# Short products that nothing reads, in the last group of a Perceiver layer, with a new planned order

## The chip, the cores and the metric

The kernel runs on one core of a Trainium2 chip. The metric is device time in microseconds: the median of several executions. The profile is one further execution, recorded by the hardware profiler. The names used below: PE is TensorE (matrix products), PEld its weight loads, DVE is VectorE, ACT is ScalarE, POOL is GpSimd and SP is SyncE, which here only issues DMAs. Each engine works through its own instructions in order; between engines they wait for each other through semaphores.

## What is computed

One Perceiver layer in float32 for 64 sequences: x is 64 × 64 × 256 and the context is 64 × 256 × 256. All three parts have a residual.

```python
def _layernorm(x, axis=-1, eps=1e-05):
    m = jnp.mean(x, axis=axis, keepdims=True)
    v = jnp.var(x, axis=axis, keepdims=True)
    return (x - m) / jnp.sqrt(v + eps)
...
x = x + _L0_xattn_ref(_layernorm(x), ctx_1024, ctx_1024, Wq, bq, Wk, bk, Wv, bv, Wo, bo)
x = x + _L0_attn_ref(_layernorm(x), w_qkv, b_qkv, w_out, b_out)
x = x + _L0_ffn_ref(_layernorm(x), w_gate, w_up, w_down)
```

The first part is cross-attention with 16 heads of 16: q from x, k and v from the context, softmax(q kᵀ / 4) v, then Wo and bo. The second is causal self-attention with the same heads. The third is a feed-forward net with quantized operands: weights are rounded to −1, 0, 1 times a scale, and activations to 8 bits with a scale per token:

```python
def _act_quant(x):
    scale = 127.0 / jnp.clip(jnp.max(jnp.abs(x), axis=-1, keepdims=True), 1e-05)
    xq = jnp.clip(jnp.round(x * scale), -128.0, 127.0) / scale
    return x + jax.lax.stop_gradient(xq - x)
...
gate = jax.nn.silu(_bitlinear(x, w_gate))
up = _bitlinear(x, w_up)
return _bitlinear(gate * up, w_down)
```

## The kernel before

The 64 sequences are worked in nine groups: seven of eight and, at the end, two of four (GB; NG is their number). A group of eight is four tiles of 128 tokens, a group of four is two. Cross-attention goes by pairs of sequences, since one context load (cT, 512 KB) holds two. Self-attention and the feed-forward net go by groups. The groups overlap: while one is in its feed-forward net, the next ones are in their attentions.

No loop sets the order of instructions. The functions describe operations (`op`) with an engine, an estimated duration, a due time `at`, and the buffers that they read and write. `Graph.run` then places them one by one, before the kernel is built: for each engine it takes the ready operation with the lowest due time, with small penalties for waiting (LATE), for a change of PE's mode (STICK) and for another ACT table (TURN), among those not further than AHEAD past the oldest operation not yet placed. SHIFT adds a fixed number to the due times of operations of one kind ("PE sc", "DVE hq f"), and LAST adds another past the due time END. For loads it reckons a landing time from their size. The result is a fixed order on every engine, and a fixed order of DMA issues on SP. Nothing is decided while the kernel runs. DMAs are dealt in turn to eight semaphore lanes, and an issue waits until the earlier DMA of its lane has landed. ACT issues the small loads at the start (bk_c, ident, par, qpar, bq_c, sel, bqk_c, causal, two bv_c, two brow); SP issues the rest.

What the steps below touch:

- The start. `load_x` (L357), `load_weights` (L361) and `load_ctx` (L366) issue from SP. PE runs 20 rows of products of ones (L939) that nothing reads, then k_a (L484, context times Wk), v_a (L519, context times Wv), tp_a (L470, transposes of the normalized x) and q_a (L484).
- A norm. `stats` (L433, L434) on DVE for each tile, giving mv; `root` (L443 to L451), eight short instructions on POOL, giving rstd and newton; `apply` (L459) on ACT for each tile, giving xn; then transposes on PE.
- `out_bias` (L367) works out the bias that goes with Wo: a DVE copy of the bv_c column into rep_bo (L372), two products on PE, and a DVE addition. `add_bias` (L550, POOL) adds it to x.
- Cross-attention for a pair: sc (L607, PE), its row maximum nm (L620, DVE), msl and mtp, scT (L638 and L643, PE), the exponentials PT (L648, ACT), av (L656, PE), keep (L677, L679, DVE).
- Self-attention: ssc (L725, PE); then, for each of two head halves and four j, mask (L737, DVE), smax (L740, DVE), less (L742, POOL), sexp (L744, ACT), stot (L748, DVE), over (L752, POOL), stp (L760, PE), spT (L765, ACT); then sav (PE), o_s (L541, PE) and x with its statistics (L545, L433, DVE).
- Feed-forward: root and apply as above; `scales` (amax_x, qunit_x, qscale_x, units; L819 to L858) and `rounded` (L862) on DVE; q (L869, DVE); its transposes qtp (L836, PE) and qT (L840, ACT). For each tile of tokens and each half of the 1024 columns: gate and up (L882, PE), silu (L889, ACT), h (L892, DVE). Then amax_hf (L819), hscaled (h_f, L908, ACT), hq (L911, DVE), hqtp (PE), hqT (ACT), down (L919, PE), x (L923, DVE). After the last tile of a group, SP stores it (L930).

PE tiles that hold products lie in PSUM: "mm" is a ring of four slots, `tile_of` takes one.

Of the kernel before, what the change touches and what calls it, by code (L numbers as in the profile page):

```python
# [39 lines left out]
P = 128  # L40
D = 256
H = 16
E = D // H
KC = D // P
# [3 lines left out]
T = 64  # L48
# [3 lines left out]
NG = len(GB)  # L52
# [43 lines left out]
class Op:  # L96
# [12 lines left out]
SETTLE = {"PE": 230.0, "ACT": 180.0, "DVE": 150.0, "POOL": 100.0, "SP": 0.0}  # L109
SELF = {"PE": 0.0, "ACT": 120.0, "DVE": 118.0, "POOL": 120.0, "SP": 0.0}  # L110
MODE = 93.0
STICK = 0.0005
TABLE = 1283.0
AHEAD = 5.691
HURRY, SPURT = 2.4886, 8
WAIT = 578031
LATE = 0.0129
TURN = 2.8858
WARM = 10
TURNS = 2  # L120

SHIFT = {
    "ACT exp": -0.11, "ACT hqT f": -10.14, "ACT hscaled f": 1.99, "ACT k s": 0.18, "ACT keep": -0.9,
    "ACT mT": 1.22, "ACT norm a": 0.11, "ACT norm f": -2.03, "ACT norm s": 2.98, "ACT q s": -0.85,
    "ACT qT f": -11.74, "ACT sexp s": -0.59, "ACT silu f": -0.43, "ACT skeep s": 1.07, "ACT spT s": -3.21,
    "ACT turned a": -1.44, "ACT v a": -2.48, "ACT v s": -0.49, "DVE h f": 0.9, "DVE hq f": 0.13,
    "DVE hscales f": 1.37, "DVE mask s": 0.027, "DVE nm": 0.73, "DVE q f": 2.75, "DVE ratio": 0.51,
    "DVE rounded f": 3, "DVE smax s": 0.07, "DVE stats a": -2.45, "DVE stats f": -3.39, "DVE stot s": 0.805,  # L130
    "DVE wdown sums": 1.47, "DVE x a": -1.84, "DVE x f": 1.05, "DVE x s": 1.31, "PE av": -0.29,
    "PE down f": -0.64, "PE gate/up f": 0.1, "PE k a": 0.05, "PE mtp": 0.12, "PE q a": -0.24,
    "PE q s": 0.03, "PE sav s": -1.58, "PE sc": -0.38, "PE ssc": -0.13, "PE stp s": 0.21,
    "PE turn a": -0.11, "PE turn s": -1.7, "PE v a": -0.1, "PE v s": 2.11, "PE wgate total": 0.98,
    "POOL less s": -1.59, "POOL root a": 2.36, "SP load wgate": 1.56, "SP load wup": 1.17,
    "SP load x": -6.63,
}

LAST = {
    "ACT exp": -2.03, "ACT hqT f": 9.14, "ACT hscaled f": 1.51, "ACT keep": -0.53, "ACT mT": -2.79,  # L140
    "ACT norm s": -5.27, "ACT qT f": 9.17, "ACT sexp s": -1.13, "ACT silu f": 1.38, "ACT spT s": 2.36,
    "ACT v a": 3.26, "ACT v s": 1.58, "DVE h f": -0.28, "DVE hq f": 1.39, "DVE hscales f": 1.92,
    "DVE mask s": -1.27, "DVE nm": -2.37, "DVE q f": -2.35, "DVE ratio": 1.17, "DVE rounded f": -1.88,
    "DVE smax s": 0.59, "DVE stats f": 1.64, "DVE stats s": 2.35, "DVE stot s": -0.66, "DVE syT s": -0.92,
    "DVE x f": 2.71, "DVE x s": -2.93, "PE down f": 3.91, "PE gate/up f": 0.21, "PE hqtp f": 2.44,
    "PE k a": 3.27, "PE mtp": 1.86, "PE o s": -2.39, "PE sc": -0.79, "PE ssc": -1.18, "PE stp s": -0.27,
    "PE v a": -1.05, "PE v s": -1.66, "POOL less s": 2.66,
}
END = 59.061


def kind(eng, name):
# [4 lines left out]
class Graph:  # L157
# [52 lines left out]
    def run(self, emit=True):  # L210
# [8 lines left out]
        for o in self.ops:  # L219
            if o.chain[0] is o:  # L220
                heads[o] = outside(o)
                if not heads[o]:
                    able[o.eng].append(o)
        table, mode, landed = None, "", 0.0
        waiting = sorted(self.ops, key=lambda o: o.at)
        done, first, order = set(), 0, []

# [24 lines left out]
        while len(done) < len(self.ops):  # L252
            while waiting[first] in done:
                first += 1
            limit = waiting[first].at + AHEAD
            best = None
            for e, ops in able.items():
                found = [(t, o) for t, o in ((start(o), o) for o in ops if o.at <= limit)
                         if t is not None]
                if not found:  # L260
                    continue
                soon = min(t for t, _ in found)
                t, o = min(((t, o) for t, o in found if t <= soon + WAIT),
                           key=lambda f: f[1].at + LATE * (f[0] - soon)
                           + STICK * (e == "PE" and f[1].mode != mode)
                           + TURN * (e == "ACT" and f[1].table not in (None, table)))
                if best is None or t < best[0]:
                    best = t, o
            if best is None:
                raise RuntimeError("no operation can go: " + ", ".join(  # L270
                    o.name for ops in able.values() for o in ops))
            t, head = best
            able[head.eng].remove(head)
            for o in head.chain:
                done.add(o)
                t = max(t, o.ready)
                for b in o.uses:
                    if b.slot is None and b.ring:
                        b.ring.to_come -= 1
                        f, _, k, b.ring = slots(b)[0]  # L280
                        t = max(t, f)
                        b.ring.held[k], b.slot = b, k
                        if emit:
                            b.t = b.ring.make(k, b)
                ns = o.ns
                if o.table and o.table != table:
                    table = o.table
                    ns += TABLE
                if o.eng == "PE" and o.mode != mode:
                    mode = o.mode  # L290
                    ns += MODE
                end = t + ns
                if o.bytes:
                    landed = max(landed, t + 1900.0) + o.bytes / 330.0
                for n in o.after:
                    seen = landed if o.bytes else end + (SELF if n.eng == o.eng else SETTLE)[o.eng]
                    n.ready = max(n.ready, seen)
                    n.missing -= 1
                    if n.chain is not o.chain:
                        h = n.chain[0]  # L300
                        heads[h] -= 1
                        if not heads[h]:
                            able[h.eng].append(h)
                for b in o.uses:
                    b.users -= 1
                    b.end = max(b.end, landed if o.bytes else end + SETTLE[o.eng])
                    if b.ring and not b.users:
                        b.ring.free[b.slot] = b.end
                o.start, o.end = t, end
                order.append(o)  # L310
                if emit:
                    o.emit()
                t = end
            free[head.eng] = t
# [12 lines left out]
def dve(n):  # L327
    return 65.0 + 1.044 * n


def pool(n):
    return 20.0 + 1.92 * n


def layers(nc, a, out, R, c):

    g_ = Graph()
    op = g_.op
# [11 lines left out]
    def tile_of(name, dtype=F32):  # L350
        return bufs("mm", [P, 512 if dtype == F32 else 1024], name, dtype)
# [7 lines left out]

    def load_weights(at, w, name):  # L360
        op("SP", 60, at, f"load {name}", lambda: nc.sync.dma_start(w.t, a[name]), writes=[w],  # L361
           size=KC * D * 4 * P)

    def load_ctx(bp, at):
        cT = cTs[bp] = bufs("cT", [P, KC, 2 * S], f"cT_{bp}")
# [182 lines left out]
    def add_bias(at, x, bias, i0):  # L548
# [3 lines left out]
            ALU.add), reads=[bias] + [(x, i) for i in range(i0, i0 + k)],  # L552
           writes=[(x, i) for i in range(i0, i0 + k)])


    def prepare(g, at, width):

# [129 lines left out]
    def self_attention(g, at, width):  # L687
        nm, x, yTa = f"s{g}", xs[g], yTs[g]
# [44 lines left out]
        def softmax(hg, j, sc, t, k):  # L733
# [5 lines left out]
                c["causal"].unsqueeze(1).to_broadcast(full), ALU.add), reads=[sc], writes=[t])  # L739
            op("DVE", dve(nt), p(k), f"smax {nm}", lambda: nc.vector.tensor_reduce(  # L740
                mx.t, t.t, AX.X, ALU.max), reads=[t], writes=[mx])
            op("POOL", pool(nt), p(k), f"less {nm}", lambda: nc.gpsimd.tensor_tensor(  # L742
                t.t, t.t, mx.t.unsqueeze(2).to_broadcast(full), ALU.subtract), reads=[mx], writes=[t])
            op("ACT", act(nt) + 40, p(k + .5), f"sexp {nm}", lambda: nc.scalar.activation(  # L744
# [2 lines left out]
            def total():  # L747
                nc.vector.reduce_sum(tot.t, t.t, axis=AX.X)  # L748
                nc.vector.reciprocal(tot.t, tot.t)

            op("DVE", dve(nt) + 218, p(k + 1), f"stot {nm}", total, reads=[t], writes=[tot])
            op("POOL", pool(nt), p(k + 1), f"over {nm}", lambda: nc.gpsimd.tensor_tensor(  # L752
                t.t, t.t, tot.t.unsqueeze(2).to_broadcast(full), ALU.mult), reads=[tot], writes=[t])

# [45 lines left out]
        for hg in range(KC):  # L800
            k = 12 + 5 * hg
# [41 lines left out]
    def ffn(g, mv, at, width):  # L843
        nm, x = f"f{g}", xs[g]
        ni = x.shape[1]
        (wg, g_unit), (wu, u_unit), (wd, d_unit) = (weights[k] for k in ("gate", "up", "down"))
        p = lambda k: at + width * k / 14
        y = root(p(0), mv, ni, nm)
        xn = bufs("xn", [P, ni, D], f"xn_{nm}")
        for i in range(ni):  # L850
            apply(p(1), x, y, xn, i, nm)
        (amax, scale, unit), emit_scale = row_scale(xn, ni, f"x{g}")
        u = bufs("units", [P, 2, ni], f"units_{g}")

# [5 lines left out]
        def rounded():  # L860
# [4 lines left out]
        q = bufs("q", [P, ni, D], f"q_{nm}", BF16)  # L865
        op("DVE", dve(ni * D) + 680, p(2), f"scales {nm}", scales, reads=[xn, g_unit, u_unit],
           writes=[amax, scale, unit, u])
        op("DVE", ni * 262, p(2.2), f"rounded {nm}", rounded, reads=[scale], writes=[xn])
        op("DVE", 40 + ni * 140, p(2.4), f"q {nm}", lambda: nc.vector.tensor_scalar(  # L869
            q.t, xn.t, MAGIC, 127.0, ALU.subtract, ALU.min), reads=[xn], writes=[q])  # L870

# [248 lines left out]
```

## Time and profile before

| | us |
|---|---|
| three runs | 861.82, 861.9, 863.13 |
| median | 861.9 |
| the profiled execution | 862.48 |
| its span | 860.7 |
| PE busy | 831.4 |
| DVE busy | 690.3 |
| ACT busy | 590.4 |
| POOL busy | 301.0 |

The profiled execution's time of 862.48 holds its span, 860.7, and 1.8 us that lie outside the records. Its mean granted TensorE clock is 0.99 of full speed. A busy share is an average over the whole span, so the profile is read by stretches. In a line of the timeline the first number is the start in us, the second the duration, then follow engine, line of the code, operation, output<-input, sizes and how many instructions the row holds; in brackets is the idle time ahead of it and what ended that.

### The profile page before, as it was taken

How to read it: one execution, taken by the hardware profiler on the slowest of the kernel's cores; microseconds unless marked ns; L12 is line 12 of the kernel's file. 1: busy time of each engine (PE TensorE's matmuls, PEld its weight loads, DVE VectorE, ACT ScalarE, POOL GpSimd, SP SyncE). 2: the span in 40 equal slices, each digit the busy share in tenths (PEclk: the TensorE clock that was granted, in tenths of full speed). 3: DMA queues.
4: the chain of work that ended last, by engine and by line, in shares of the span. 5: the costliest groups of instructions: out<-in, count | busy, mean ns of one | idle time of the engine just before them, and what ended most of it. 6: DMA issues, size and time to landing. Idle time of an engine off the chain costs nothing. (4 is left out here: it accounts for less than half of the span.)

```text
span 860.7 us, 28167 instructions
## 1 busy us (share of the span) xinstructions
PE 831.4 (97%) x12136; PEld 573.2 (67%) x12136; DVE 690.3 (80%) x1499; ACT 590.4 (69%) x948; POOL 301.0 (35%) x505
## 2 busy tenths in 40 slices
PE   8999899999999999999999999999999999998966
PEld 5766657776577756676667766777567775776633
DVE  2587678896888878988789886889779877999995
ACT  3554666547986597747886487865888487767855
POOL 3330527424242334405144152422344141354640
PEclk9999999999999999999999999999999999999988
DMA  7212201002022210222112111211012320011110
GB/s 264 76 51 100 75 27 51 27 3 62 14 51 64 57 40 6 51 88 39 38 38 51 39 39 39 50 58 51 8 39 51 64 38 14 14 27 39 26 37 38
DMA packets 47740, 41.82 MB, mean 49 GB/s; under 512 B 39168, under 2 KB 39680, under 8 KB 47616
## 3 DMA queue, kind: packets, MB, share of 16 engines
q1 hardware_dynamic: 45888, 39.59, 17.5%
q8 instruction: 95, 1.56, 0.7%
q10 hardware_dynamic: 1728, 0.43, 0.2%
q14 instruction: 29, 0.24, 0.1%
HBM read 26.65 MB, written 4.19 MB: 36 GB/s over the span
## 5 line engine op out<-in xcount | busy, mean ns | idle before, releaser
L620 DVE TENSOR_REDUCE nm<-sc 128x8 f32<-128x2048 f32 x64 | 144.7, 2261 | 27.9 <-PE sc L607 27.9
L648 ACT ACTIVATE PT<-scT 128x1024 f32<-128x1024 f32 x128 | 125.1, 1020 | 28.4 <-PE scT L643 28.1
L484 PE MATMUL k_a<-cT,wk 128*128 128x512 f32 x256 | 122.7, 609 | 2.5 <-DMA wk<-in_wk_dram 2.5
L519 PE MATMUL v_a<-wv,cT 128*128 128x256 f32 x512 | 122.6, 383 | 0.0
L682 POOL TENSOR_TENSOR yT_a<-keep 128x128 f32<-128x128 f32 x64 | 30.7, 480 | 247.7 <-DVE keep L679 189.0
L519 PEld LDWEIGHTS v_a<-wv,cT 128*128 128x128 f32 x512 | 95.0, 190 | 19.6 <-issue 3.2
L742 POOL TENSOR_TENSOR s_s<-s_s,smax_s 128x512 f32<-128x512 f32 (+1 forms) x72 | 67.3, 951 | 60.5 <-DVE smax_s L740 56.8
L507 ACT ACTIVATE kT<-k_a,bk_c 128x512 f32<-128x512 f32 x64 | 43.9, 685 | 59.4 <-PE k_a L484 59.1
L656 PEld LDWEIGHTS av<-PT,v 128*32 128x32 f32 x4096 | 60.4, 110 | 28.6 <-ACT PT L648 13.0
L484 PEld LDWEIGHTS k_a<-cT,wk 128*128 128x128 f32 x256 | 46.4, 192 | 47.5 <-issue 39.0
L752 POOL TENSOR_TENSOR s_s<-s_s,stot_s 128x512 f32<-128x512 f32 (+1 forms) x72 | 67.1, 952 | 27.6 <-DVE msl L613 12.3
L607 PE MATMUL sc<-kT,qm 32*128 32x256 f32 x1024 | 73.3, 400 | 3.0 <-ACT PT L648 3.0
L643 PE MATMUL scT<-qm,kT 32*128 32x128 f32 x2048 | 75.1, 270 | 0.0
L677 DVE SCALAR_TENSOR_TENSOR keep<-av,par,keep 128x256 f32<-128x256 f32 x64 | 30.6, 479 | 53.6 <-ACT keep L672 43.7
L656 PE MATMUL av<-PT,v 128*32 128x64 f32 x4096 | 71.4, 221 | 2.0 <-ACT PT L648 1.8
L643 PEld LDWEIGHTS scT<-qm,kT 32*128 32x128 f32 x2048 | 68.5, 186 | 0.2
L679 DVE RECIPROCAL keep<-keep 128x128 f32<-128x128 f32 x64 | 61.0, 953 | 2.2
L607 PEld LDWEIGHTS sc<-kT,qm 32*128 32x128 f32 x1024 | 46.2, 184 | 19.8 <-ACT PT L648 5.8
L737 DVE TENSOR_TENSOR s_s<-ssc,causal 128x512 f32<-128x512 f32 (+1 forms) x72 | 42.7, 620 | 13.4 <-PE ssc L725 13.2
L892 DVE SCALAR_TENSOR_TENSOR h_f<-up_f,units,silu_f 128x512 f32<-128x512 f32 x64 | 46.5, 739 | 7.7 <-ACT silu_f L889 6.3
L550 POOL TENSOR_TENSOR x<-x,bo_r 128x512 f32<-128x512 f32 x32 | 40.1, 1272 | 32.6 <-issue 16.7
L525 ACT COPY v<-v_a 128x512 f32<-128x512 f32 x64 | 37.2, 582 | 20.9 <-PE v_a L519 20.8
(156 smaller groups left out, 1677.6 us busy)
## 6 DMA issues: line engine op xcount, KB each, us to landing
cT<-in_ctx_dram SPq DMA_DIRECT2D x32, 512.0 KB, 3.4
x<-in_x_dram SPq DMA_DIRECT2D x7, 512.0 KB, 3.7
out_dram<-x SPq DMA_DIRECT2D x7, 512.0 KB, 2.8
wffn_gate<-in_wgate_dram SPq DMA_DIRECT2D x2, 512.0 KB, 5.8
wffn_up<-in_wup_dram SPq DMA_DIRECT2D x2, 512.0 KB, 5.7
wffn_down<-in_wdown_dram SPq DMA_DIRECT2D x2, 512.0 KB, 3.7
wqkv<-in_wqkv_dram SPq DMA_DIRECT2D x1, 768.0 KB, 7.4
x<-in_x_dram SPq DMA_DIRECT2D x2, 256.0 KB, 2.6
```

What stands on the lines that cost most here:

```text
L484: nc.tensor.matmul(pm.t[:, 0:n], w.t[:, kc, c0:c0 + P], src.t[:, kc, :], start=(kc == 0), stop=(kc == KC - 1))
L507: op("ACT", act(n) + 100, at, f"k {name}", lambda: nc.scalar.activation(kT.t[:, hg, :], pm.t[:, 0:n], AF.Identity, bias=bias), reads=[pm], ...
L519: nc.tensor.matmul(pm.t[:, i * D:(i + 1) * D], src.t[:, kc, (i0 + i) * P:(i0 + i + 1) * P], w.t[:, kc, c0:c0 + D], start=(kc == 0), stop=( ...
L607: nc.tensor.matmul(sc.t[:, j, hg, :], q(hg, j), kT.t[rows(j), hg, k0:k0 + S], start=True, stop=True)
L620: op("DVE", dve(NJ * KC * S), at, f"nm {n}", lambda: nc.vector.tensor_reduce(nm.t, sc.t, AX.X, ALU.max, negate=True), reads=[sc], writes=[nm])
L643: nc.tensor.matmul(sT.t[:, j, hg, s * P:(s + 1) * P], kT.t[rows(j), hg, k0 + s * P:k0 + (s + 1) * P], q(hg, j), start=False, stop=True, sk ...
L648: op("ACT", act(NJ * S), at + .03, f"exp {n}", lambda: nc.scalar.activation(pT.t[:, hg].rearrange("p j k n -> p j (k n)"), sT.t[:, :, hg, ...
L656: nc.tensor.matmul(av.t[rows(j), h, hg, :], v.t[:, ((n % 2) * SC + s) * NP + hg * NJ + j, 2 * h:2 * h + 2, :].rearrange("p a e -> p (a e)" ...
L679: nc.vector.reciprocal(t.t[:, 1], t.t[:, 1])
L742: op("POOL", pool(nt), p(k), f"less {nm}", lambda: nc.gpsimd.tensor_tensor(t.t, t.t, mx.t.unsqueeze(2).to_broadcast(full), ALU.subtract), ...
L752: op("POOL", pool(nt), p(k + 1), f"over {nm}", lambda: nc.gpsimd.tensor_tensor(t.t, t.t, tot.t.unsqueeze(2).to_broadcast(full), ALU.mult), ...
L892: op("DVE", dve(512) + 60, p(k), f"h {nm}", lambda: nc.vector.scalar_tensor_tensor(h.t[:, n0:n0 + 512], up.t, u.t[:, 1, i:i + 1], sl.t, AL ...
```

## The change

A new function makes one PE operation of one product of the identity with a value that another engine has just made (the row maxima or sums of a softmax, or a mean and variance, an inverse root, a normalized tile, a scale), and of four bf16 products of 128 × 128. They go to a "mm" tile that nothing reads. It is called in the last group alone: in self-attention after smax and after stot for even j (eight times), and in the feed-forward net after mv, after the root, after xn, after the scales and after the rounding (five times). That makes 13 operations and 65 products.

```diff
+BRIDGE = 4
...
+    def kept_warm(at, name, src, rhs):
+
+        pt = tile_of(f"warm_{name}_{len(g_.ops)}")
+
+        def emit():
+            nc.tensor.matmul(pt.t[:, 0:rhs().shape[-1]], c["ident"], rhs(), start=True, stop=True)
+            for k in range(BRIDGE):
+                nc.tensor.matmul(pt.t[:, P:2 * P], c["sel"][:, 0, :], c["ident16"], start=True, stop=True)
+
+        op("PE", 330, at, f"bridge {name}", emit, reads=[src], writes=[pt])
...
+            if g == NG - 1 and j % 2 == 0:
+                kept_warm(p(k), nm, mx, lambda: mx.t)
...
+            if g == NG - 1 and j % 2 == 0:
+                kept_warm(p(k + 1), nm, tot, lambda: tot.t)
...
+        final = g == NG - 1
+        if final:
+            kept_warm(p(0), nm, (mv, ni - 1), lambda: mv.t[:, ni - 1, :])
...
+        if final:
+            kept_warm(p(.5), nm, y[0], lambda: y[0].t)
+            kept_warm(p(1.5), nm, (xn, ni - 1), lambda: xn.t[:, ni - 1, 0:T])
...
+        if final:
+            kept_warm(p(2.1), nm, scale, lambda: scale.t)
...
+        if final:
+            kept_warm(p(2.3), nm, xn, lambda: xn.t[:, ni - 1, 0:T])
```

The planner is told other numbers. The load of wqkv is counted with its real size, three times what it was; the first landing is reckoned from 3,000 ns on, and the rate is 300 bytes per ns instead of 330. Its constants change a little, and all of SHIFT and LAST is new.

```diff
-STICK = 0.0005
+STICK = 0.0002
...
-AHEAD = 5.691
-HURRY, SPURT = 2.4886, 8
-WAIT = 578031
-LATE = 0.0129
-TURN = 2.8858
+AHEAD = 6.0713
+HURRY, SPURT = 2.4951, 8
+WAIT = 180501000.0
+LATE = 0.0126
+TURN = 2.8337
...
-END = 59.061
+END = 59.2063
...
-        table, mode, landed = None, "", 0.0
+        table, mode, landed = None, "", 3000.0
...
-                    landed = max(landed, t + 1900.0) + o.bytes / 330.0
+                    landed = max(landed, t + 1900.0) + o.bytes / 300.0
...
-           size=KC * D * 4 * P)
+           size=KC * (3 * D if name == "wqkv" else D) * 4 * P)
```

A few entries of SHIFT that bear on the start and the end:

```diff
-    "DVE rounded f": 3, "DVE smax s": 0.07, "DVE stats a": -2.45, "DVE stats f": -3.39, "DVE stot s": 0.805,
...
-    "SP load x": -6.63,
...
+    "DVE stats f": -1.87, "DVE stats s": 0.55, "DVE syT s": -0.1, "DVE terms": 0.65,
...
+    "SP load ctx": -3.56, "SP load wgate": 0.91, "SP load wv": -7.98, "SP load x": -7.6,
```

By the built orders of both kernels, the steady groups differ in swaps of neighbours. At the start, SP issues x, wv, cT of the first pair, cT of the second, wk, x of the second group, wq, wo, wqkv, wout, where it issued x, cT, wk, x, wv, wq, cT, wo, wqkv, wout. PE's first real products are v_a, then k_a. On DVE the two rep_bo copies stand ahead of the first group's statistics instead of behind the second group's. At the end, hq of the third tile of the group before stands ahead of the last statistics, and hq of its fourth tile behind the h products.

## The prediction

> **What bounds the kernel now.** I read the page's first part, then busy time by stretches of 20 us, then the order of events where TensorE (PE) is not full.
>
> ```profile
> PE 831.4 (97%) x12136; PEld 573.2 (67%) x12136; DVE 690.3 (80%) x1499; ACT 590.4 (69%) x948; POOL 301.0 (35%) x505
> ```
>
> ```profile
> 80.00:100.00 20.00, 18.68 (x286) 13.42 (x284) 16.06 (x35) 9.22 (x17) 9.32 (x12) 1.00 0.23 81
> 400.00:420.00 20.00, 20.00 (x258) 12.06 (x260) 14.72 (x30) 18.73 (x30) 9.10 (x18) 1.00 0.19 19
> 800.00:820.00 20.00, 17.62 (x172) 12.25 (x169) 19.31 (x56) 15.41 (x35) 13.23 (x30) 0.99 0.13 25
> 820.00:840.00 20.00, 14.34 (x121) 7.96 (x121) 18.95 (x53) 12.57 (x25) 8.23 (x20) 0.84 0.21 54
> 840.00:861.00 21.00, 12.93 (x84) 7.25 (x84) 11.78 (x21) 11.82 (x13) 0.96 (x3) 0.83 0.07 25
> ```
>
> The columns are the stretch, its length, busy PE, PEld, DVE, ACT and POOL, then the granted clock. Three regimes show. From about 20 to 740 us PE is full (20.00 of 20), so whatever delays its first real work delays the end by as much. From 740 to 840 VectorE (DVE) is the bound (18.5 to 19.3 of 20). After 840 no engine is full: one dependent chain ends the run, at a mean clock of 0.83. All of PE's idle time is 860.7 − 831.4 = 29.3 us; 12.7 of it lies after 820 (5.7 + 7.1 by the stretches).
>
> The start, from the events in order of time:
>
> ```profile
> 6.36 0.42 DVE L433 BATCH_NORM_STATS2 st_a<-x 128x6 f32<-128x256 f32 x1
> 6.69 0.83 ACTq L993 DMA_DIRECT2D bv_c<-in_bv_c_dram  x2
> 8.66 0.17 DVE L434 BATCH_NORM_AGGREGATE mv_a<-st_a 128x2 f32<-128x6 f32 x1
> 8.92 0.24 POOL L443 TENSOR_SCALAR var_a<-mv_a 128x4 f32<-128x4 f32 x1 [4.16 <-DVE mv_a L434]
> 12.05 1.09 ACT L459 ACTIVATE xn_a<-x,newton_a,rstd_a 128x256 f32<-128x256 f32 x2 [0.30 <-POOL newton_a L451]
> 12.14 0.46 DVE L372 COPY rep_bo_r<-bv_c 128x256 f32<-128x256 f32 x2
> 16.03 1.04 PE L470 MATMUL tp_a<-ident,xn_a 128*128 128x128 f32 x8
> 16.91 1.88 PE L484 MATMUL k_a<-cT,wk 128*128 128x512 f32 x4
> ```
>
> DVE takes the first group's statistics at 6.36, POOL's root runs 8.92 to 12.02, ACT's four normalizations end at 14.70, and the transposes tp_a start at 16.03, behind v_a: the norm had 1.33 us to spare. The bias copies rep_bo come after all that, at 12.14, though bv_c was issued at 6.69.
>
> The end, from the same view:
>
> ```profile
> 820.55 1.26 PE L760 MATMUL stp_s<-ident,s_s 128*128 128x128 f32 x4 [2.33 <-POOL s_s L752]
> 839.99 0.41 PE L836 MATMUL qtp_f<-ident,q_f 128*128 128x128 bf16 x4 [4.16 <-DVE q_f L869]
> 841.14 1.04 PE L882 MATMUL gate_f<-wq_gate,qT_f 128*128 128x512 bf16 x2 [0.73 <-ACT qT_f L840]
> 847.09 0.60 PE L882 MATMUL up_f<-wq_up,qT_f 128*128 128x512 bf16 x2
> 857.11 0.48 DVE L923 SCALAR_TENSOR_TENSOR x<-down_f,qunit_hf,x 128x256 f32<-128x256 f32 x1 [0.85 <-PE down_f L919]
> ```
>
> and the clock over stretches of 3.41 us, on whose edges all its changes in this trace fall:
>
> ```profile
> 816.35:819.77 3.42, 1.87 (x40) 1.46 (x36) 3.17 (x12) 0.31 (x1) 2.45 (x8) 1.00 0.02 5
> 833.42:836.83 3.41, 2.42 (x15) 1.21 (x13) 3.34 (x7) 2.19 (x4) 2.08 (x9) 1.00 0.11 22
> 836.83:840.24 3.41, 0.25 (x4) 0.23 (x4) 3.31 (x11) 0.28 (x1) 0.10 (x1) 1.00 0.38 154
> 840.24:843.65 3.41, 2.68 (x9) 0.89 (x7) 2.35 (x5) 2.41 (x3) 0.19 (x1) 0.50 0.00 0
> ```
>
> After a stretch with PE busy 55% (1.87 of 3.42) the next ran at half clock; after one with 71% (2.42) it did not. The gap of 4.16 us made the last gate/up products run at half clock until 847.0: 1.04 against 0.60 for the same row.
>
> **The change, part by part.**
>
> *Start.* The enlarged size of wqkv and the slower load model move DMAs and, with the new shifts, the order. On SP, x keeps its place, wv comes before wk, and cT of the first pair before both; wk now waits for the lane of sel, x of the second group for bqk_c's, wq for causal's. On PE v_a comes first, then k_a, then tp_a: the same work ahead of tp_a. On DVE the two rep_bo copies, which wait for both bv_c loads, now stand ahead of the first group's statistics, and these wait behind them. The bv_c loads were issued at 6.69 and 7.1 and took 3.5 and 3.6, so the second lands at 10.7. From there: copy .23 → 10.93; four statistics 2.23 (as the second group's did, 10.00 to 12.23) → 13.16; handover .09 and root 3.10 → 16.35; four normalizations, with a v_a copy of .56 where a kT copy of .67 stood, 2.7 → about 19.1; the last five of eight transposes .65 → 19.8. Before, tp_a ended at 17.07: +2.7. Bounds: a load as short as causal's 1.7 gives 8.8 for the second and +0.8; one as long as brow's 5.4 gives 12.5 and +4.5. I take bv_c's own row. wk, issued near 7.5, lands at 12.1 if it takes wv's 4.6; k_a, 3.4 without the half clock, then ends at 15.5, ahead of the norm: no charge.
>
> PE then idles about 15.5 to 17.5 and is thin until 19.1. A stretch at half clock costs 3.41/2 = 1.7, as the cold start before (7.43 to 10.85 at .51) did. That old one hides in the after kernel under the wait for wk. None, one or two new ones: 0 to +3.4. I place the idle on the 3.41 grid at all phases; in about 7 of 10 one stretch falls under 55%: +1.2.
>
> *Early groups.* one v_a tile, about 1.7 us (two took 12.58 to 16.03), now stands between mtp and av at 88 us, and covers two waits there, 1.05 and .27 on ACT's PT: −1.3. If ACT's exponentials slip with it, 0. The waits of 1.52 at 107 and .98 at 208 keep their order.
>
> *Bridges.* 13, each one short f32 product and four bf16 128×128. Nearest rows: hqtp_f, eight 128×128 bf16 in .61 (first to last start some .46), so .058 each; five make .3, in all 3.9 us of PE; each holds one of four PSUM slots until its own end. None reads late there: the eight in the softmax stand behind transposes that already waited for the same chain, in a stretch where DVE is full and PE idles 2 to 6 us of 20; without that cover they cost 2.4. The five of the FFN wait for mv, rstd, xn, scale and rounded xn. Behind mv's stand gate and up of the second tile; mv was done at 833.18 and gate ran at 833.88, so .7 spare. Behind the others stand only down_2, down_3 (x adds that have time) and qtp, which waits for the later q. Their extra price: 0 (to +0.5: one bridge late by what its chain is).
>
> *Tail.* DVE is full up to the last q_f (839.95) and has one x add (.43) less to do before it: −0.4. If the clock stays full, eight halves of gate/up save .43 each, 3.4 on PE, but then DVE's h, amax and hq set the order: by its rows (.75, 1.22, .35, .69) the last x ends near 854.85 instead of 857.59: −2.7 in all. If it is halved but released at an earlier edge, each us of release gives about .8. Between 834.9 and 838.1 only .3 to .6 us of bridges fall, and down_2 and down_3 lie at its ends; over the grid's phases some 7 in 10 have a stretch under 55%. I take one edge's partial gain: −0.8 (bounds −2.7, +0.5, if the reordered hq and x adds hold amax_x up).
>
> The Trainium skill, "TensorE: Matmul & The Clock Gate", "Part 1: The HAM clock gate", says that the clock goes cold after at least one idle window of about 3.4 us, free running; by that rule any bridge in the gap keeps it warm and the tail would give −2.7. The 55% stretch above, in which PE never idled so long, contradicts it, and the measurement decides.
>
> *All else.* The steady groups see neighbours swapped. PE is full there, so 0 ± 1.5: the largest single wait of that stretch, 1.5, may go or come.
>
> **Sum.** +2.7 +1.2 −1.3 −0.8 = +1.8. The profiled execution took 862.48 (span 860.7 and 1.8 around it), .58 over the median 861.9. So 864.3 against the profiled one, 863.7 against the median, which I forecast.
>
> **Rivals.** A measurement of this kernel can tell 0.2%, 1.7 us, from no change: 860.2 to 863.6.
> 1. *It cancels.* PE's clock stays full at the start or at the end, not at both ends lost: +2.7 +0 −1.3 −0.8 = +0.6, or +2.7 +1.2 −1.3 −2.7 = −0.1. About 862.1. For it: each is one phase draw. Against: both draws stand 7 to 3 the other way.
> 2. *Faster: the bridges hold the clock across the 4.16 us gap.* Place: gate/up at 841 to 847; price −2.7, with −1.3 at 88 us. It decides the sign once the start costs under 2.3: if the second bv_c takes bqk_c's 2.8 us it lands at 9.9, the start costs +1.9 with no half clock, and 1.9 − 1.3 − 2.7 = −2.1: 859.8. For it: the second stretch at 833 with 71% stayed warm, and down_3 in the gap adds 1.05. Against: the start's rows.
> 3. *The start is worse*: brow's 5.4 and two cold stretches, +4.5 +1.7 −1.3 −0.4 = +4.5: 866.4. Part of the slower case.
> 4. *The bridges do nothing*: clock falls as before, tail −0.4, sum +2.2: 864.1. Also slower.
>
> **Numbers.** Slower, with 3 and 4: .42, own range 863.6 to 867.0. Rival 1: .30. Rival 2: .28, 858.7 (start at its +0.8) to 860.2. These are the chances of slower, same, faster. The range reaches from 858.5 (rival 2's lower end) to 867.0 (rival 3's 866.4 with the tail's +0.5).
>
> **What would show it.** Right: rep_bo on DVE near 10.2 to 10.9 ahead of st_a; tp_a ending near 19.8; k_a of the second pair there instead of 16.91; no av wait at 88; gate_f rows of .6 or 1.04 after the last q_f tell whether the bridges held the clock. Wrong: tp_a ending before 18, wk landing after 15, or a new wait above 1 us between 100 and 740, where nothing absorbs it.

## The result, and the profile after

| | before | changed |
|---|---|---|
| median, us | 861.86 (4 runs, 861.57 to 863.13) | 870.04 (4 runs, 869.0 to 871.32) |
| ratio | 1 | 1.0093, 95% interval 1.0073 to 1.0113 |
| profiled execution: time, span | 862.48, 860.7 | 871.32, 869.5 |

The changed kernel is slower by 8.2 us, where 1.8 was forecast. The first part of its page shows six more busy microseconds on PE and about one on DVE, ACT and POOL:

```profile
span 869.5 us, 28347 instructions
PE 837.3 (96%) x12214; PEld 579.6 (67%) x12214; DVE 691.6 (80%) x1499; ACT 591.2 (68%) x948; POOL 302.0 (35%) x505
```

Of PE's six, the bridges (the new products) are 5.4: counted without their rows PE is busy 831.9. PE's idle time grew from 29.3 to 32.2 us (869.5 − 837.3). Busy time by stretches (columns as before the change, the clock third from the end) shows where PE's clock was lower:

```profile
0.00:20.00 20.00, 12.57 (x46) 8.80 (x46) 5.46 (x23) 3.73 (x6) 6.74 (x19) 0.96 0.83 279
20.00:40.00 20.00, 19.73 (x123) 12.24 (x124) 6.60 (x12) 8.93 (x16) 4.29 (x7) 0.87 0.09 33
200.00:220.00 20.00, 17.68 (x240) 11.00 (x239) 15.85 (x29) 14.43 (x25) 11.77 (x23) 0.91 0.20 58
820.00:840.00 20.00, 18.13 (x203) 13.29 (x202) 18.19 (x56) 12.29 (x29) 12.22 (x26) 0.85 0.12 23
840.00:860.00 20.00, 15.62 (x108) 9.46 (x107) 17.84 (x38) 12.74 (x17) 3.19 (x12) 0.98 0.21 53
```

The kernel before had 0.91, 1.00, 1.00, 0.84 and 0.83 in these places. So the half clock has left the last stretch, and has come to two that ran at full clock before: after 20 and at 216.

To place the loss, the starts of the 64 row maxima nm (one for each sequence, always in the same order) are compared one by one with those of the kernel before. The table gives the difference in us. Its last row compares the starts of the last x. The names of the other columns are those of the experiments below.

| nm | changed | start_alone | copies_back | undo_middle | no_bias_one | no_bias_later | best |
|---|---|---|---|---|---|---|---|
| 1st, 25.08 us before | 6.58 | 6.86 | 1.16 | 7.22 | 6.20 | 5.87 | −0.89 |
| 11th | 5.03 | 6.85 | −0.39 | 5.67 | 4.65 | 4.33 | −2.44 |
| 20th, 210.06 | 6.41 | 6.50 | 1.03 | 5.32 | 3.53 | 5.95 | −2.44 |
| 21st, 218.61 | 8.27 | 6.51 | 2.94 | 5.32 | 3.75 | 7.57 | −2.43 |
| 60th, 712.36 | 10.64 | 6.48 | 5.34 | 7.95 | 5.87 | 6.81 | −1.94 |
| 64th, 769.99 | 9.43 | 6.48 | 4.37 | 6.73 | 4.63 | 5.67 | −2.50 |
| last x, 857.11 | 8.87 | 5.84 | 3.93 | 3.95 | 3.90 | 3.23 | −5.22 |

Read down the second column: 6.6 us are lost before the first nm, 1.6 come back by the 11th, 5.6 are lost between the 11th and the 60th, and 1.8 come back at the end. Each column is one execution (that of the changed kernel is its slowest), but the loss between the 11th and the 60th nm is 5.4 to 5.7 in all four profiles that keep the new order there (changed, undo_start, copies_back, no_bridges). The waits of PE name the places:

```profile
PE mtp L637 <- DVE msl L628: 5.1, 5, 2.3
PE tp_a L471 <- ACT xn_a L460: 3.2, 2, 2.7
```

Neither line stood near the top before: mtp waited 1.0 us once, tp_a not at all.

### The profile page after: what moved, and what is told of

Read it like the earlier page. It is cut to its first block, busy times and chain, and to the rows that moved or that the text cites. A ratio compares the mean times of both kernels' runs of the same rounds, so it can differ in the third digit from the quotient of the medians.

```text
span 869.5 us, 28347 instructions
## 1 busy us (share of the span) xinstructions
PE 837.3 (96%) x12214; PEld 579.6 (67%) x12214; DVE 691.6 (80%) x1499; ACT 591.2 (68%) x948; POOL 302.0 (35%) x505
## 3 DMA queue, kind: packets, MB, share of 16 engines
q1 hardware_dynamic: 45888, 39.59, 16.7%
## 4 chain that ended last, share of the span: by engine, by line
PE 75%; DVE 13%; ACT 5%; POOL 2%; issue 2%; DMA 0%; ACTq 0%; DVEq 0%; POOLq 0%
PE k_a L485 10%; PE v_a L520 10%; PE sc L619 6%; PE av L668 6%; PE scT L655 5%; PE ssc L737 3%; PE q_a L485 3%; PE stp_s L776 3%; PE v_s L520 3%; PE o_s L542 3%; PE q_s L485 3%; PE down_f L945 3%; PE gate_f L908 3%; PE o_a L542 3%; DVE nm L632 3%; PE up_f L908 2%
## 5 line engine op out<-in xcount | busy, mean ns | idle before, releaser
L915 ACT ACTIVATE silu_f<-gate_f,units 128x512 f32<-128x512 f32 x64 | 43.5, 686 | 10.6 <-PE gate_f L908 10.3
L684 ACT ACTIVATE keep<-av,par 128x256 f32<-128x256 f32 x64 | 30.6, 479 | 25.9 <-PE av L668 25.1
```

## Experiments

Most kernels here keep all operations and change only their planned order. The order is given as a list of the operations' numbers, cut and joined from the orders of the two kernels at places where both have done the same set of operations. The places used lie ahead of the 56th, 319th, 628th, 889th and 2483rd operation (about 24, 105, 205, 280 and 735 us), which makes six pieces. The edit is the same for all:

```diff
-        while len(done) < len(self.ops):
-            while waiting[first] in done:
...
-            t, head = best
+        for k in PLACES:
+            head = self.ops[k]
+            if head.chain[0] is not head:
+                continue
+            t = max(start(head), free[head.eng])
             able[head.eng].remove(head)
```

Times are compared with the kernel before, run on the same chip beside them (861.9 to 862.5).

### Each part alone: start and bridges

undo_start: first piece old, the rest as changed.

> The changed kernel with the old order of its first 55 planned operations (loads, DVE copies, k_a and v_a; up to the first nm), everything later as changed. Theory: the first nm came 6.58 us later (25.08 to 31.66) and PE is full behind it, so the loss passes through: 870.0 - 6.6 = 863.4, between 862 and 865; first nm at 25.1. Rival (the loss is absorbed before the end, and the later order costs the 8 us): 868 to 870.

Measured: 863.3, ratio 1.0016 (1.0006 to 1.0027). The loss of the start passes through to the end.

start_alone: first piece new, the rest old, no bridges.

> The kernel before with the new order of its first 55 planned operations alone, no bridges. Theory: 861.9 + 6.6 = 868.5, between 867 and 869.5. Rival (absorbed): 862 to 864.

Measured: 868.27, ratio 1.0069 (1.0057 to 1.0081). The first nm comes 6.86 late and the 64th 6.48: nothing in between takes it back. The two runs agree on 6 to 7 us for the start.

no_bridges: the changed order, and nothing issued for the bridges.

```diff
     def kept_warm(at, name, src, rhs):
+        return
```

> The changed kernel with nothing issued for its 13 bridges, all other operations in the same order. Theory: the bridges hold the clock over the last norm, so without them the last gate and up rows go from .59 to 1.04 us and the end comes 1 to 2.7 us later: 871 to 872.7. Rival (the bridges' 3.9 us of PE and their waits cost more than they save): 866 to 869.5.

Measured: 872.76, ratio 1.0119 (1.0106 to 1.0132) against 1.0093 (1.0073 to 1.0113) with them. The two intervals overlap a little, with four executions each. The mean clocks are 0.988 to 0.990 without the bridges and 0.989 to 0.994 with them, and the profiles show a saving at the end. Two stretches of 3.41 us around the last norm, between edges of the clock, first with bridges, then without:

```profile
847.70:851.11 3.41, 1.94 (x20) 1.64 (x20) 3.27 (x11) 2.01 (x3) 0.19 (x1) 1.00 0.41 77
851.11:854.53 3.42, 3.23 (x29) 1.95 (x27) 3.21 (x8) 1.44 (x3) 0.19 (x1) 1.00 0.32 132
```

```profile
848.26:851.68 3.42, 1.05 (x8) 0.70 (x8) 3.25 (x11) 1.81 (x3) 0.19 (x1) 1.00 0.42 81
851.68:855.09 3.41, 3.20 (x17) 1.84 (x18) 2.59 (x6) 1.20 (x2) 0.19 (x1) 0.50 0.37 154
```

The 1.05 without bridges is one row of down products, which both have. The bridges raise PE's share from 31% (1.05) to 57% (1.94), and the next stretch keeps its clock. From the last q_f to the last x it then takes 14.8 us (851.16 to 865.98); without bridges 16.0 (851.41 to 867.38); in the kernel before, with two halved stretches, 17.6. So of the 2.8 us against the kernel before, 1.2 go with the bridges. They do not always hold the clock: of the eight profiles with this tail and the bridges, five ran the last gate rows at full clock (14.8 each) and three lost one stretch (undo_start, no_bias_one, best_warm: 16.1 to 16.3).

bridges_alone: the old order, with the bridges put in at the same neighbours on PE where a free buffer allowed it.

> The kernel before with the 13 bridges put into its PE order, nothing else changed. Theory: clock held at the last gate and up, 861.9 less 1 to 2.7: 859.2 to 861. Rival (the bridges delay PE in the DVE-bound stretch or do not hold the clock): 862 to 865.

Measured: 861.68, ratio 0.9996 (0.9987 to 1.0005): no change that can be told. Yet its twelve executions ran at mean clocks of 0.994 to 0.998, those of the kernel before beside them at 0.990 to 0.994. The bridges did keep more of the clock, and it brought no time; why was not found. In its profile the first two of the last gate rows still take 1.04 and 1.06. In the old order the last down product of the group before (837.41) stands ahead of four of the FFN's bridges, where in the changed kernel it stands between them, and PE has less in that gap. That this is the reason was read from the order and not tried by itself.

### The start: loads or copies

copies_back: the changed order with two DVE operations moved.

```diff
 DVE order at the start
-rep_bo_r, rep_bo_r, stats of group 0, stats of group 1
+stats of group 0, stats of group 1, rep_bo_r, rep_bo_r
```

> The changed kernel with only the two rep_bo copies moved back behind the second group's statistics on DVE; the new order of loads and of PE stays. Theory (the copies' wait for bv_c holds the first norm up): the norm is ready before k_a ends near 16.0, first nm near 26 instead of 31.66, 864 to 865.5. Rival (the new order of loads and PE is what costs): 868.5 to 870.

Measured: 863.04, ratio 1.0015 (1.0003 to 1.0027), the first nm only 1.16 late. The order in time of the changed kernel, and under it that of copies_back:

```profile
7.16 0.82 ACTq L1019 DMA_DIRECT2D bv_c<-in_bv_c_dram  x2
12.50 0.29 DVE L373 COPY rep_bo_r<-bv_c 128x256 f32<-128x256 f32 x1 [0.54 <-DMA bv_c<-in_bv_c_dram]
12.71 0.42 DVE L434 BATCH_NORM_STATS2 st_a<-x 128x6 f32<-128x256 f32 x1
18.14 1.09 ACT L460 ACTIVATE xn_a<-x,newton_a,rstd_a 128x256 f32<-128x256 f32 x2 [7.22 <-POOL newton_a L452]
18.79 0.97 PE L471 MATMUL tp_a<-ident,xn_a 128*128 128x128 f32 x2 [2.75 <-ACT xn_a L460]
21.87 3.50 PE L485 MATMUL k_a<-cT,wk 128*128 128x512 f32 x4
```

```profile
4.95 0.42 DVE L489 BATCH_NORM_STATS2 st_a<-x 128x6 f32<-128x256 f32 x1
16.97 0.46 DVE L428 COPY rep_bo_r<-bv_c 128x256 f32<-128x256 f32 x2
17.19 1.04 PE L526 MATMUL tp_a<-ident,xn_a 128*128 128x128 f32 x8
```

The statistics begin at 12.71 behind the copies, and at 4.95 without them. With the copies behind, tp_a no longer waits for xn_a. In the changed kernel the four k_a products behind tp_a take 3.50, where they took 1.88 before: half clock. The loads' new order stays in both, so by itself it does not cost: copies_back ends 0.5 us above the kernel before, undo_start with the old loads 1.0.

copies_alone: the old order with the two copies ahead.

> The kernel before with only the two copies moved ahead of the first group's statistics. Theory: the second bv_c lands near 10.7 there, so the first nm comes 2.7 us later, and up to 2 more where PE's clock falls in the gap: 864.5 to 866.5, less than the 868.3 of the whole new start, the rest being bv_c's later landing under the new loads. Rival (the loads alone cost): 861.5 to 862.5.

Measured: 866.12, ratio 1.0057 (1.0044 to 1.007). The copies alone give 3.6 us, most of the 5.9 of start_alone; the other 2.3 come with the new loads and PE's new order behind the copies. Here too the second bv_c landed late, and its copy began at 11.96, not 10.7. In the nine profiles with the old order of loads it landed between 10.4 and 12.4, in the seven with the new one between 12.1 and 13.9: what nobody had waited for before was no sure time.

### The steady groups: POOL's additions beside DVE's short steps

undo_middle: pieces three and four (105 to 280 us) old, the rest as changed.

> The changed kernel with the old order between about 105 and 280 us (operations 318 to 888 of the plan). Theory (POOL's bias additions run beside DVE's short msl steps there and make mtp wait 2.32 instead of .98, with a stretch at half clock behind it): 870.0 - 3.1 = 866.9, between 865.8 and 868. Rival (that stage only passes on a delay from earlier): 869.5 to 870.5.

Measured: 868.38, ratio 1.0075 (1.0062 to 1.0088), by the medians 1.7 less (2.3 when each is taken against the kernel before beside it). That lies between the ranges of the theory and of the rival. In the table the delay no longer rises at the 20th and 21st nm (5.32 in both). So the stage makes its own delay; the medians show less of it than the 3.1 expected.

What waits there is mtp, for DVE's last msl step. The kernel before, on POOL, DVE and PE:

```profile
201.31 1.27 POOL L550 TENSOR_TENSOR x<-x,bo_r 128x512 f32<-128x512 f32 x1 [1.32 <-ACT xn_s L459]
204.48 3.72 POOL L550 TENSOR_TENSOR x<-x,bo_r 128x512 f32<-128x512 f32 x3
206.62 0.38 DVE L613 SCALAR_TENSOR_TENSOR msl<-nm 128x8 bf16<-128x8 f32 x1
207.04 1.19 DVE L614 SCALAR_TENSOR_TENSOR nm<-msl,nm 128x8 f32<-128x8 bf16 x1
208.69 0.23 PE L625 MATMUL mtp<-ident,msl 128*128 128x128 bf16 x1 [0.98 <-DVE msl L616]
```

The changed kernel on DVE, POOL and PE:

```profile
211.50 0.90 DVE L625 SCALAR_TENSOR_TENSOR msl<-nm 128x8 bf16<-128x8 f32 x1
212.43 1.19 DVE L626 SCALAR_TENSOR_TENSOR nm<-msl,nm 128x8 f32<-128x8 bf16 x1
213.65 1.19 DVE L627 SCALAR_TENSOR_TENSOR msl<-nm 128x8 bf16<-128x8 f32 x1
214.87 0.17 DVE L628 SCALAR_TENSOR_TENSOR msl<-msl,nm 128x8 bf16<-128x8 bf16 x1
```

```profile
209.87 4.94 POOL L551 TENSOR_TENSOR x<-x,bo_r 128x512 f32<-128x512 f32 x4
```

```profile
215.10 0.23 PE L637 MATMUL mtp<-ident,msl 128*128 128x128 bf16 x1 [2.32 <-DVE msl L628]
216.35 1.03 PE L908 MATMUL up_f<-wq_up,qT_f 128*128 128x512 bf16 x2
```

Four additions of about 1.24 us follow each other from 209.87, and the last three end near 212.3, 213.6 and 214.8. The first three steps, 128 × 8 each, end at 212.40, 213.62 and 214.84, each with an addition. The fourth comes after them and takes 0.17. In the kernel before, one addition ran ahead of the chain, and two steps met one.

Meetings as such are not new. Of the 256 msl steps (four for each sequence) 21 take over 0.23 us in the kernel before and 15 in the changed one, and above 0.17 each they cost DVE 11.8 and 11.3 us. What is new is that they fall together: three in one chain at 211, and 0.89 with 1.19 at 314, 416 and 517, each ahead of a wait of mtp (2.32, and 0.72 to 0.73). The kernel before has single ones there (0.89 at 306, 0.39 at 311) and no wait.

no_bias_one and no_bias_later leave additions out of the changed kernel (here the first):

```diff
-            add_bias(p(6), x, bo_r, i0)
+            add_bias(p(6), x, bo_r, i0, g in (3,))
...
-            add_bias(p(16), x, bo2_r, i0)
+            add_bias(p(16), x, bo2_r, i0, g in (1,))
```

> The changed kernel without four of POOL's bias additions (bo_r of group 3, bo2_r of group 1: the four that run from 209.87 to 214.81). Theory (DVE's short msl steps each wait for the end of such an addition): the steps that took .90, 1.19 and 1.19 us take .17, mtp's wait of 2.32 goes to under .3, the half clock behind it goes, and the delay against the kernel before from nm 21 on is 3 to 4 us less: 866 to 867.5. Rival (nm itself is late there): wait stays above 1.5, 869 to 870.5.

Measured: 866.93, ratio 1.0057 (1.0042 to 1.0071). DVE in the same place:

```profile
211.11 0.17 DVE L625 SCALAR_TENSOR_TENSOR msl<-nm 128x8 bf16<-128x8 f32 x1
211.31 0.17 DVE L626 SCALAR_TENSOR_TENSOR nm<-msl,nm 128x8 f32<-128x8 bf16 x1
211.52 0.17 DVE L627 SCALAR_TENSOR_TENSOR msl<-nm 128x8 bf16<-128x8 f32 x1
211.72 0.17 DVE L628 SCALAR_TENSOR_TENSOR msl<-msl,nm 128x8 bf16<-128x8 bf16 x1
```

All four take 0.17, this wait of mtp is gone (its longest is now 0.7, elsewhere), and the 21st nm comes 3.75 late instead of 8.27.

> The changed kernel without the bias additions of the four later places (bo_r of groups 4 to 7, bo2_r of groups 2 to 5), the ones at 210 left in. Theory: the four waits of mtp of .6 to .7 us go, and with them the slow growth of the delay by some .5 us a group: 2.0 to 2.8 less, 867.2 to 868. Rival (the growth comes from the swaps on PE): 869.5 to 870.5.

Measured: 866.27, ratio 1.0049 (1.0037 to 1.0061), 0.9 us below the range that was expected. From the 21st to the 60th nm the delay no longer grows (7.57 to 6.81). The four short waits of mtp, 2.8 us together, were that growth of 2.4.

before_no_bias is the control.

> Control: the kernel before without the same twenty bias additions (bo_r of groups 3 to 7, bo2_r of groups 1 to 5). Theory: in its order the additions make mtp wait only once (.98 at 208), so leaving them out gives .5 to 1.5 us: 860.8 to 861.8. Rival (the additions cost wherever they stand, and the new order does not matter): 857 to 859, as much as in the changed kernel.

Measured: 861.27, ratio 0.999 (0.9981 to 0.9999), 0.8 less than the kernel before. (By count the operations left out are nineteen.) The same additions cost 0.8 us in the old order, and by the sum of the two runs above some 6.9 in the new one (7.6 when each is taken against the kernel before beside it; the two were not run together). The order costs, not the additions.

### A mixed order

best: pieces one, three, four and five old, two and six new, with the bridges.

> Old order at the start, new from 24 to 105 us, old from 105 to 740, new after that with the 13 bridges. Theory: 861.9 less 1.5 (the av waits at 88) less 1.8 (the tail): 858.6, between 857.5 and 860. Rival (the gains of the new stages depend on the delay they were planned for): 861 to 863.

Measured: 860.11, ratio 0.9973 (0.9962 to 0.9984). It beats both kernels, by 2.4 and about 10 us, but less than expected. Its ten executions range from 857.22 to 861.53, the profiled one being the fastest, so its column in the table, with its start 0.89 early, shows a lucky one.

> The mixed order without its 13 bridges, all else as there. Theory: the last gate and up fall to half clock again as in the changed kernel without bridges: 860.0 + 1.5 to 2.7 = 861.5 to 862.7. Rival (the mixed order's gain is its order alone): 859.5 to 860.5.

Measured: 859.84, ratio 0.9976 (0.9966 to 0.9987), the same as with the bridges. So in the mixed order the gain is the order's alone, and the expectation fell. Its mean clocks are 0.992 to 0.994, with the bridges 0.994 to 1.0, and in its profile one of the last gate rows still takes 1.06. So the bridges keep some clock here too, and by the medians it brings nothing; where the time goes was not found.

before_warm and best_warm: more products of ones at the very start.

```diff
-WARM = 10
+WARM = 16
```

> The kernel before with 16 products of ones at the start instead of 10, which keep PE busy until near 7.2 when wk lands. Theory: executions in which k_a starts at half clock lose 1.7 us by it, and no longer do: 860.8 to 861.5. Rival (the cold start hides behind x's norm and the loads): 861.9 to 862.8.

> The mixed order (old start, new from 24 to 105 us, old to 740, new after that with the bridges) with 16 products of ones instead of 10. Theory: as before_warm, 1 to 1.7 less than the 860.1 of the mixed order: 858.4 to 859.2, with less spread. Rival: 860 to 860.8.

Measured: 863.13, ratio 1.0012 (1.0003 to 1.002), and 859.78, ratio 0.9975 (0.9965 to 0.9984). Both expectations fell. In before_warm's profile k_a runs at full clock (3.70 instead of 5.40), but now PE waits for wv behind it (until 13.2), and the half clock comes from 13.3 to 16.7 instead. The loss moved.

## Why the prediction was wrong

**The side was right, and the mechanism of the start.** rep_bo stood ahead of st_a, and tp_a came late, as the prediction said. The term was mis-sized. It took +2.7 with bv_c landing at 10.7, from a row in which nothing waited for it. It landed at 12.5 in the changed kernel, which the prediction had as its upper bound, +4.5. tp_a ended at 22.07, not 19.8: +5.0. The half clock was put at +1.2 and fell on two stretches (18.3 to 25.1). Both together are 6.6 at the first nm, where 3.9 was forecast; start_alone gives 5.9 by the medians.

**The early groups** were right: −1.3 forecast, −1.6 measured between the first and the 11th nm, and the two waits at 88 are gone.

**"All else ... 0 ± 1.5" is the step that failed.** It argued that the steady groups only see neighbours swapped and that PE is full there. The runs show 5.6 us lost between the 11th and the 60th nm. The new order moved POOL's additions in time, so that up to three in a row run beside the DVE steps that PE's next product waits for, and the wait of 2.3 us was followed by a stretch at half clock as well (in no_bias_one neither is there). Not all of it is swaps of neighbours: POOL converts wq_down (two instructions of 2.77 us) at 191.78 and 197.66, where the kernel before does it from 133.23. Whether that is what pushes the four additions together at 210 was not tried by itself. The prediction looked at each engine's own order and not at what runs at the same moment on another. It had the wait at 208 among its rows, .98 long, and said that it would keep its order. The wait stayed at its place and grew to 2.32, which is what the prediction itself named as a sign of being wrong: a new wait above 1 us between 100 and 740.

**The bridges and the tail.** −0.8 was forecast with the clock not kept. The clock was kept (.59 to .61 for each of the last gate rows). The price for that case was right: the last x came 2.8 us sooner after the last q_f, where the prediction worked out 2.7. But 1.6 of the 2.8 stay without the bridges, and that the clock was kept is in part luck: three of the eight profiles with this tail and the bridges lost a stretch. The bridges' work was put at 3.9 us of PE and is 5.4. And from the 64th nm to the last q_f the changed kernel took 2.2 us longer (71.7 against 69.5), while its first gate rows of the group before ran at 1.04 in a half-clock stretch from 834 to 840.9. In undo_middle, where no such stretch shows, the same part takes 69.5. From the 60th nm to the last x, 1.8 came back.

**Rivals.** That it would cancel, or that the bridges would make it faster, fell with the start: even its gains of 1.6 and 1.8 do not reach the 6.6. The worse start was nearest: its 4.5 for the load and 1.7 for the clock make 6.2, close to the 6.6, but its 866.4 is still short by the steady groups.

**The sum.** Forecast: +2.7 +1.2 −1.3 −0.8 and 0 for the steady groups, +1.8. The two profiles show +6.6 −1.6 +5.6 −1.8, +8.8. Two slips in the working change nothing: PE's idle time after 820 is 13.4, not 12.7 (the last stretch holds 20.7 us of span), and rival 2's lower end is 858.7 in one place and 858.5 in another.

The Trainium skill, "SBUF — State Buffer", section "Who interferes with whom", says that a VectorE instruction with two inputs in SBUF contends with a GpSimd instruction that reads SBUF, since its second input comes through the read interface that both share, and that the order of issue decides who blocks. The msl rows agree: 0.90, 1.19 and 1.19 us with additions running, 0.17 without. In the 16 profiles 272 msl steps take over 0.23 us; each of them overlaps a POOL instruction, and 266 end within 0.06 us after one ends. This page bore on the change and the prediction did not weigh it.

## What to carry to other kernels

A swap that looks harmless on one engine can move a long instruction of another engine beside a short one that shares something with it. Compare the orders across engines at the places where the bound engine has its longest waits, even if those waits look fixed. A copy that waits for a load must not stand ahead of the first work of the critical chain in an in-order queue; a landing time for which nobody has waited yet is an estimate, not a bound. Where a full PE follows a gap, count the half clock behind the gap with the gap.

## What the runs showed of the hardware

- The clock can fall after a stretch of 3.41 us that is partly busy; no whole idle stretch is needed. In the changed kernel the stretch from 212.84 to 216.25 was busy 34% and the next one ran at half clock. In the 16 profiles every stretch at full clock with PE busy under 48% was followed by half clock, and over 60% only one was (83%, in undo_start before 813.3). Between the two the share as this profile counts it does not decide: in the changed kernel one of 55% (830.63 to 834.05) was followed by half clock, one of 57% (847.70 to 851.11) and one of 49% (857.96 to 861.38) were not. The page cited in the prediction asks for an idle window; here too the measurement differs.
- Release takes a busier stretch: the one from 834.05 to 837.46, at half clock and busy 94%, was followed by another at half clock; the one after it was full, and was followed by full clock. In the 16 profiles every full stretch at half clock was followed by full clock and none under 85% was; between them both happen (86% in before_no_bias was enough).

```profile
212.84:216.25 3.41, 1.15 (x17) 0.82 (x17) 2.13 (x3) 1.19 (x3) 1.97 (x2) 1.00 0.35 135
216.25:219.67 3.42, 3.42 (x9) 1.47 (x6) 3.17 (x4) 1.37 (x2) 0.00 (x0) 0.50 0.00 0
830.63:834.05 3.42, 1.88 (x19) 1.31 (x17) 3.25 (x12) 1.20 (x4) 2.26 (x4) 1.00 0.00 0
834.05:837.46 3.41, 3.22 (x43) 2.00 (x42) 2.98 (x7) 1.85 (x5) 0.95 (x3) 0.50 0.03 7
837.46:840.87 3.41, 3.41 (x9) 1.87 (x8) 2.05 (x5) 3.38 (x5) 0.19 (x1) 0.50 0.00 0
857.96:861.38 3.42, 1.67 (x16) 1.15 (x16) 3.35 (x7) 2.68 (x4) 0.39 (x1) 1.00 0.02 5
861.38:864.79 3.41, 2.96 (x32) 2.29 (x32) 1.85 (x5) 2.91 (x3) 0.19 (x1) 1.00 0.08 29
```

- Where these stretches begin against the kernel's start differs from execution to execution: the kernel before ran k_a at half clock in its profile, the mixed order, with the same start, at full. The changed kernel's four runs are 869.0 and 869.06 at a mean clock of 0.994, and 871.02 and 871.32 at 0.992 and 0.989. Single kernels spread by 4 to 5 us (best 857.2 to 861.5, undo_start 861.5 to 866.9), about as much as the effects that were looked for.
